# Products with v five rounds behind, another order of buffers, and side pieces from round 6 on

## The chip, the core and the metric

The kernel runs on one core of one Trainium2 chip. The metric is the time on the device in microseconds (us), as the median of several executions. The core's engines work side by side, each through its own queue in order: PE (TensorE), DVE (VectorE), ACT (ScalarE), POOL (GpSimd) and SP (SyncE, which here only issues transfers).

## The reference

Two layers on N = 3327 nodes with D = 128 features and a sparse adjacency matrix adj of zeros and ones. Layer 0 is a graph attention; layer 1 is an attention for each of the D features, with 8 components per node (H = 8), and takes by far most of the time.

```python
H = X @ W.T + b;  s = H @ a_s;  r = H @ a_r
e = leaky_relu(A * s + A * r.T, 0.2)
att = softmax(where(A > 0, e, -9e15), axis=1)
x = layernorm(X + att @ H)                        # layer 0

q, k, v = ((x @ W.T).reshape(d, n, h) for W in (Wq, Wk, Wv))
a = einsum('dnh,dmh->dnm', q, k) * d ** -0.5
a = softmax(a + adj + adj, axis=2)
out = einsum('dnm,dmh->dnh', a, v)
x = layernorm(x + out.reshape(n, h * d) @ Wo.T)   # layer 1
```

## The kernel before

**Layer 1.** The features are taken four at a time (HG = 4): 32 groups. The 3327 queries are cut into 7 blocks of 476 columns (the last has 472); so there are 224 blocks, counted through. The keys are 26 tiles of 128 (or 127) rows. For each key tile the kernel computes the scores of the four features (L152, written to PSUM tiles scb that hold two features), applies the exponential and the adjacency, and multiplies with v (L956), adding up in one PSUM tile av. After the 26th key tile of a block VectorE copies av to SBUF (L966), and SP writes it out (L970).

**Two ways to the weights.** The adjacency stands in the exponent as 0 or 2. Half a key tile (two features, 952 columns) goes one of two ways. Either ScalarE takes exp of the scores from PSUM (L1172), and GpSimd multiplies the result with a factor of 1 or e squared (L1173). Or VectorE adds adjacency and scores (L1175), and ScalarE takes exp of the sum later (L991, function exp_late): in the round after the sum is complete, for the whole key tile, 1904 columns. Both write into a tile e4 of the pool sp, which has seven buffers that are given out in turn.

**Rounds.** A block has NR = 26 rounds; one round handles two halves. Three key tiles make a triple of three rounds: in the first and the second, one half goes through ScalarE and GpSimd (tile i) and one through VectorE (tile k1); in the third, both halves of tile k2 go through VectorE. I call these rounds A, B and C. Blocks alternate between two plans. An even block starts with a triple (rounds 0, 1, 2 are A, B, C) and ends with rounds 24 and 25 for the last two tiles. An odd block starts with a round of VectorE alone (round 0), its triples begin at rounds 1, 4, 7 and so on, and round 25 handles one tile alone, one half each way.

**The order of a round.** The kernel writes out the order of each engine's queue by hand (a manual schedule). A round puts on the queues: SP's adjacency loads for a later stretch (want_adj); PE's scores; at most one side piece for PE (work_tensor); the halves on ScalarE and GpSimd or on VectorE; the late exponentials that are due; the products of one key tile (function multiply); and side pieces for VectorE and GpSimd (work). The function multiply keeps a list of key tiles whose product has not been issued, and issues the oldest when there are more than LAG = 4: products run four rounds behind. So the last product of a block, and the copy L966 that follows it, are issued in round 3 of the next block. The scores of ScalarE's half use the PSUM pool pe with one buffer, those of VectorE's half the pool pd with two, av the pool pv with one.

In odd blocks the products of round 3 are issued between the two halves on VectorE:

```python
between = odd and n == LAG - 1
...
if between and h == 1:
    multiply(s, order[n])
```

**Side pieces.** Layer 0 of the other 25 row tiles and the projections of the results are cut into small pieces that run beside layer 1. They stand in two rows: "main" (products of layer 0, L241, its normalisation, and the projections to q, k, v, and the pieces of the results) and "aside" (GpSimd's weights, L308 and L317, the loads of their adjacency, and VectorE's counts, L326). Each piece has a kind: "p" for PE, "d" and "l" for VectorE, "m" for GpSimd, "x" for loads that take no slot; "n" waits for a mark that "t" sets. The functions reading and lane say in which rounds of a block a kind has a slot, for one piece each: before, PE, VectorE and GpSimd have slots in rounds 4, 7, 10 and so on (second rounds of triples), in some first and last rounds, and PE in round 3 too (in odd blocks all one later); "l" has them a round later. The function finish_to runs what is left when a group of features needs its rows.

Of the kernel before, what the change touches and what calls it, by code (L numbers as in the profile page):

```python
# [17 lines left out]
P = 128  # L18
# [29 lines left out]
def kernel(  # L48
# [29 lines left out]
    H = wqT.shape[1]  # L78
# [13 lines left out]
    kr = [FP + (i < N - FP * NT) for i in range(NT)]  # L92
# [57 lines left out]
    def special():  # L150
# [9 lines left out]
        with ExitStack() as sx, tc.manual_schedule(engines=ALL):  # L160
# [9 lines left out]
            CH = [(i, min(i + CW, NT)) for i in range(0, NT, CW)]  # L170
# [96 lines left out]
            def layer0(t, side=True, trow=None, bank=bank, held=None):  # L267
# [4 lines left out]
                r = rows[t]  # L272
                s = {"a": {}, "w": {}}
# [191 lines left out]
                for n, (i0, i1) in enumerate(CH):  # L465

                    aside.append(("n", ("P", q0 + n - 2, 0)))
                    for c0 in range(i0, i1, 3):
                        c1 = min(c0 + 3, i1)
                        aside.append(("m", lambda n=n, c0=c0, c1=c1: weigh(n, c0, c1)))  # L470
                        aside.append(("m", lambda n=n, c0=c0, c1=c1: mask(n, c0, c1)))
                    aside.append(("t", ("W", q0 + n)))
                    c = [("d", lambda n=n, h=h, k=k: count(n, h, k)) for h in range(3) for k in range(2)]
                    counts.append(c)
                    main.append(("n", ("W", q0 + n, 3)))
                    if i1 == NT:
                        main.append(("m", biased))
                    main += [("p", lambda i=i: product(i)) for i in range(i0, i1)] + [("t", ("P", q0 + n))]
                    aside.append(counts[-1])
                return loads, main + chain + [("t", ("rows", t))], aside  # L480

            def result(t):
# [116 lines left out]
                units += [("p", lambda: turn(0, 2, 0)), ("p", lambda: turn(2, 4, 2))]  # L599
                units += [("d", lambda: divided(0, 2, 0)), ("d", lambda: divided(2, 4, 2))]  # L600
                units += [("p", lambda: turn(4, 5, 0)), ("d", lambda: divided(4, 5, 0))]
                units += [("p", lambda h=h: project(h)) for h in range(H)]
                root = rsqrt(s, lambda: s["st"][:r, 7:8], r)
                units += [("d", finish), ("d", together(variance, *root[:3]))]
                return units + [("d", together(*root[c : c + 3])) for c in (3, 6, 9)] + [("d", scale)]
# [314 lines left out]
            pd = sx.enter_context(tc.tile_pool(name="sx_sd", bufs=2, space=bass.MemoryType.PSUM))  # L920
            pe = sx.enter_context(tc.tile_pool(name="sx_se", bufs=1, space=bass.MemoryType.PSUM))
            pv = sx.enter_context(tc.tile_pool(name="sx_av", bufs=1, space=bass.MemoryType.PSUM))
            LAG = 4

# [47 lines left out]

            waiting = []

            def multiply(s, i):
                waiting.append((s, i))
                while len(waiting) > LAG:
                    products(*waiting.pop(0))  # L980

# [20 lines left out]

            def reading(n, odd):

                n -= odd
                if n % 3 == 1 and 4 <= n < NR - 2:  # L1010
                    return True
                return n in ((NR - 2,) if odd else (0, NR - 1))

            def lane(kind, n, odd):

                if kind == "l":
                    return int(reading(n - 1, odd) if n else True)
                return int(reading(n, odd) or kind == "p" and n - odd == 3)

            made = [layer0(t) for t in range(1, NT)]  # L1020
            first_loads = made[0][0]
            main = []
            aside = []
            for n, (_, m, a) in enumerate(made):

                later = []
                for u in a:
                    if u[0] == "r":

                        at = max((k for k, v in enumerate(aside) if v[0] == "n"), default=0)  # L1030
                        aside.insert(at, ("x", u[1]))
                    elif isinstance(u, list):
                        ahead = made[n + 1][0][sum(isinstance(v, list) for v in later)] if n + 1 < len(made) else None
                        later.append(u)
                        if n:
                            aside += u + [ahead] * (ahead is not None)
                    else:
                        aside.append(u)
                if n == 0:

                    for k, u in enumerate(later):
                        aside += u + [made[1][0][k]] * (len(made) > 1)
                main.append(m)
            main.append([("n", ("counts", 0, 0))] + judge())
            aside.append(("t", ("counts", 0)))
            results = [((needs[t] + 1) * total + LAG + 6, result(t)) for t in range(NT - 1)]
            end = result(NT - 1)
            marks = {("P", q): 0 for q in range(len(CH))}
            side = {"main": [], "aside": aside, "since": {"main": 0, "aside": 0}, "read": -2}

            def head(row, now, force=False):

                while True:
                    if not side[row]:
                        if row == "aside":
                            return None
                        ahead = ("rows", reads[min(max(now, 0) // total + 2, NG - 1)]) in marks
                        if results and results[0][0] <= now and (ahead or not main):
                            side[row] = results.pop(0)[1]
                        elif main:  # L1060
                            side[row] = main.pop(0)
                        else:
                            return None
                    kind, f = side[row][0]
                    if kind == "t":
                        marks[f] = now
                    elif kind == "w":
                        if not force and now - side["since"][row] < f:
                            return None
                    elif kind == "n":  # L1070
                        if f[:2] not in marks or not force and now - marks[f[:2]] < f[2]:
                            return None
                    else:
                        return kind
                    side[row].pop(0)
# [4 lines left out]

            def work_tensor(now, n, odd):

                for _ in range(lane("p", n, odd) if side["read"] != now - 1 else 0):
                    if head("main", now) != "p":
                        break
                    run("main", now)

            def work(now, n, odd):
                room, low, pool = lane("d", n, odd), lane("l", n, odd), lane("m", n, odd)
                for row in ("main", "aside"):  # L1090
                    while True:
                        kind = head(row, now)
                        if kind == "x":
                            pass
                        elif kind == "d" and room:
                            room -= 1
                            if row == "main":
                                side["read"] = now
                        elif kind == "l" and low:
                            low -= 1  # L1100
                            side["read"] = now
                        elif kind == "m" and pool:
                            pool -= 1
                        else:
                            break
                        run(row, now)

            def finish_to(mark, now):
                while mark not in marks:
                    row = "main" if head("main", -1 if now is None else now, True) else "aside"  # L1110
                    if head(row, -1 if now is None else now, True) is None:
                        break
                    run(row, -1)
                    tick(True)
# [13 lines left out]
            for g in range(NG):  # L1128
                k4, v4, _ = group
                for b in range(NBLK):  # L1130
# [5 lines left out]
                    for n, rnd in enumerate(rounds):  # L1136
# [22 lines left out]
                            for t in range(2):  # L1159
                                pair_scores(sc[i, h][: kr[i], t, :w], s.k4, s.q4, i, kr[i], 2 * h + t, w)  # L1160
                        work_tensor(g * total + at, n, odd)
                        between = odd and n == LAG - 1
                        for (i, h, at_) in rnd:
                            if between and h == 1:
                                multiply(s, order[n])
                            r, z = kr[i], sc[i, h]
                            if i not in s.e:
                                s.e[i] = sp.tile([P, HG, WB], F32, name="e4")
                            eh = s.e[i][:r, 2 * h : 2 * h + 2, :w]
                            ah = a[:r, at_ or 0, :w].unsqueeze(1).to_broadcast([r, 2, w])  # L1170
                            if at_ is None:
                                nc.scalar.activation(eh, z[:r, :, :w], AF.Exp, scale=2.0)  # L1172
                                nc.gpsimd.tensor_tensor(eh, eh, ah, op=ALU.mult)  # L1173
                            else:
                                nc.vector.tensor_tensor(eh, z[:r, :, :w], ah, op=ALU.add)  # L1175
                                added.setdefault(i, []).append(h)
# [5 lines left out]
                        if n + 1 in starts or n + 1 == NR:  # L1182
                            del adjs[m]
                            make_factor(m + 1)
                        if not between:
                            multiply(s, order[n])
                        work(g * total + at, n, odd)
            exp_late(NG * total + 2)
            finish_to(None, NG * total + LAG + 6)
# [384 lines left out]
```

## Time and profile before

| | before |
|---|---|
| median of 3 runs | 10047.68 us (10047.55 to 10053.35) |
| profiled execution, its own time | 10052.42 us |
| its span | 10050.6 us |
| first exponential of layer 1 starts | at 66.3 us |
| last exponential of layer 1 ends | at 10025.3 us |
| granted TensorE clock, mean | 0.995 |
| stretch from 114 to 167 us (53 us), busy: PE, DVE, ACT, POOL | 41.9, 40.1, 45.8, 51.2 us |
| stretch from 4972 to 5017 us (45 us), the same | 43.0, 39.9, 44.8, 44.4 us |

The page gives each engine's busy time and its share of the span, and then groups of instructions: line, engine and operation, output and inputs by name, shape and count; behind the bar the busy time in us and the mean ns of one, then the idle time of the engine before them and what ended most of it. A line of waits gives who waited for whom, the sum in us, how often, and the longest. A line of the timeline gives start, duration, engine, line, operation, names, shapes and how many instructions were merged, and in brackets the idle time before it and what ended it. A busy share counts overlapping instructions once.

### The profile page before, as it was taken

Reading aid. Unit: us, or ns where it says so; the run is one execution under the profiler, and the core shown is the slowest. Engines: PE = TensorE matmul, PEld = TensorE weight load, DVE = VectorE, ACT = ScalarE, POOL = GpSimd, SP = SyncE. Lnnn points to the kernel's source line nnn. Section 1 sums busy time; section 2 is a strip of 40 time slices with the busy share of each in tenths; the row PEclk is TensorE's granted clock in tenths of the full one; section 3 lists DMA queues with packets and bytes.
Section 4 is the critical chain, followed back from the end, with each engine's and each line's share of the span. In section 5 each row is a group of like instructions: output and inputs, shape, how many; then the busy total and the mean of one; then the engine's idle time right before and its main releaser. Section 6 shows DMA issues by size and latency. Waiting matters only on the chain.

```text
span 10050.6 us, 207550 instructions
## 1 busy us (share of the span) xinstructions
PE 9477.4 (94%) x79523; PEld 3013.9 (30%) x79523; DVE 9188.5 (91%) x10554; ACT 9897.6 (98%) x7904; POOL 9177.2 (91%) x4954
## 2 busy tenths in 40 slices
PE   7999999999999999999999999999999999999998
PEld 2233333333233233323333333333333233222222
DVE  7899999999999999999999999999999999888888
ACT  7999999999999999999999999999999999999998
POOL 7999999999999999999999999999999999888887
PEclk9999999999999999999999999999999999999999
DMA  6765656665665656565566656566665565555554
GB/s 194 209 179 179 179 168 183 178 176 168 181 173 171 183 167 189 168 184 170 169 179 187 176 172 179 176 170 178 181 179 175 171 175 168 169 158 166 164 164 132
DMA packets 1399414, 1755.28 MB, mean 175 GB/s; under 512 B 349360, under 2 KB 1386890, under 8 KB 1394312
## 3 DMA queue, kind: packets, MB, share of 16 engines
q1 hardware_dynamic: 1388061, 1739.30, 59.7%
q8 instruction: 626, 10.26, 0.4%
q10 hardware_dynamic: 10347, 2.61, 0.1%
q14 instruction: 380, 3.11, 0.1%
HBM read 1637.49 MB, written 103.93 MB: 173 GB/s over the span
## 4 chain that ended last, share of the span: by engine, by line
ACT 41%; PE 21%; POOL 16%; issue 13%; DVE 7%; DMA 2%; SPq 1%; POOLq 0%; ACTq 0%; DVEq 0%
ACT e L991 29%; POOL e L1173 15%; ACT e L1172 11%; PE av L956 11%; PE scb L152 9%; DVE e L1175 5%; PE bank L241 1%; DVE o L966 1%; DMA q4b<-qT 1%; DMA at<-in_adjT_dram 1%; POOL w L308 0%; SPq L733 0%; POOL w L317 0%; DMA k4b<-kT 0%; POOL at L793 0%
## 5 line engine op out<-in xcount | busy, mean ns | idle before, releaser
L1173 POOL TENSOR_TENSOR e<-e,at 128x952 f32<-128x952 f32 (+1 forms) x3920 | 8715.9, 2236 | 788.6 <-ACT e L1172 735.1
L1175 DVE TENSOR_TENSOR e<-scb,at 128x952 f32<-128x952 f32 (+1 forms) x7728 | 8499.4, 1142 | 769.7 <-PE scb L152 650.1
L991 ACT ACTIVATE e<-e 128x1904 f32<-128x1904 f32 (+3 forms) x3920 | 7095.9, 1810 | 26.4 <-DVE e L1175 11.1
L956 PE MATMUL av<-e,v4b 128*32 128x476 f32 (+1 forms) x46592 | 5843.8, 573 | 99.0 <-DVE o L966 68.0
L152 PE MATMUL scb<-q4b,k4b 32*128 32x476 f32 (+1 forms) x23296 | 3882.4, 486 | 440.8 <-ACT e L1172 361.9
L1172 ACT ACTIVATE e<-scb 128x952 f32<-128x952 f32 (+1 forms) x3920 | 3921.1, 1000 | 74.9 <-PE scb L152 36.7
L152 PEld LDWEIGHTS scb<-q4b,k4b 32*128 32x128 f32 (+1 forms) x23296 | 1779.3, 189 | 5459.2 <-ACT e L1172 3161.5
L956 PEld LDWEIGHTS av<-e,v4b 128*32 128x32 f32 (+1 forms) x46592 | 1014.1, 109 | 1239.9 <-issue 933.4
L241 PE MATMUL bank<-hsb,w 128*32 128x129 f32 (+1 forms) x5200 | 278.6, 286 | 0.0
L326 DVE TENSOR_SCALAR_CACHE_REDUCE dump<-a 128x384 bf16<-128x384 f32 (+2 forms) x468 | 247.3, 528 | 0.6
L308 POOL TENSOR_SCALAR w<-trow,er 128x129 f32<-128x129 f32 x650 | 231.6, 376 | 1.3
L317 POOL TENSOR_TENSOR w<-w,a 128x384 f32<-128x384 f32 (+3 forms) x225 | 207.9, 924 | 0.1
L966 DVE COPY o<-av 128x476 f32<-128x476 f32 (+1 forms) x224 | 145.2, 648 | 31.3 <-PE av L956 30.4
L241 PEld LDWEIGHTS bank<-hsb,w 128*32 128x32 f32 (+1 forms) x5200 | 102.9, 108 | 148.2 <-issue 148.2
L241 PE MATMUL bank<-wo,ot 128*32 128x128 f32 x1600 | 85.2, 285 | 0.0
L402 DVE TENSOR_SCALAR hi<-bank 128x256 fp32r<-128x256 f32 (+1 forms) x200 | 83.0, 415 | 0.0
L409 DVE SCALAR_TENSOR_TENSOR lo<-bank,hi 128x256 fp32r<-128x256 f32 (+1 forms) x200 | 83.0, 415 | 0.0
L241 PE MATMUL bank<-wk,x1T 128*32 128x256 f32 x800 | 63.9, 391 | 0.0
L241 PE MATMUL bank<-wq,x1T 128*32 128x256 f32 x800 | 63.9, 391 | 0.0
L241 PE MATMUL bank<-wv,x1T 128*32 128x256 f32 x800 | 63.9, 391 | 0.0
L502 PE MATMUL bank<-ident,o 128*128 128x128 f32 x225 | 52.0, 304 | 0.0
L290 POOL MEMSET a<- 128x128 f32 (+1 forms) x25 | 5.2, 208 | 44.4 <-DVE dump L326 44.4
(123 smaller groups left out, 647.3 us busy)
## 6 DMA issues: line engine op xcount, KB each, us to landing
at<-in_adjT_dram SPq DMA_DIRECT2D x1536, 476.0 KB
at<-ftd SPq DMA_DIRECT2D x1674, 238.0 KB
at<-in_adjT_dram SPq DMA_DIRECT2D x256, 472.0 KB
at<-ftd SPq DMA_DIRECT2D x279, 236.0 KB
k4b<-kT SPq DMA_DIRECT2D x128, 415.9 KB
q4b<-qT SPq DMA_DIRECT2D x1528, 29.8 KB
at<-in_adjT_dram SPq DMA_DIRECT2D x192, 208.2 KB
at<-in_adjT_dram SPq DMA_DIRECT2D x150, 238.0 KB
```

The costliest lines, as they stand in the source:

```text
L152: nc.tensor.matmul(dst, k4[32 * j : 32 * j + H4, first_key(i) : first_key(i) + 2 * r - 1 : 2], q4[32 * j : 32 * j + H4, :nb], start=True, ...
L241: nc.tensor.matmul(dst[c0:c1], w[:, c0:c1], mov, **kw)
L308: nc.gpsimd.tensor_scalar(w, s["t"][:, :, :T3], -LOWEST, e, op0=ALU.min, op1=ALU.max)
L317: nc.gpsimd.tensor_tensor(w, w, s["a"][n][:, c0 - i0 : c1 - i0, :r], op=ALU.mult)
L326: nc.vector.tensor_scalar(z, a, float(k), None, op0=ALU.is_equal, op1=ALU.add, accum_out=even[:, t, at : at + 1])
L402: nc.vector.tensor_scalar(hi[:r, o : o + QW], s["b"][:r, :QW], scale, None, op0=ALU.mult)
L956: nc.tensor.matmul(s.av[32 * j : 32 * j + 32, : s.w], s.v4[:r, j, i * H1 : i * H1 + 32], e[:r, j, : s.w], start=(s.left == NT - 1), stop=( ...
L966: nc.vector.tensor_copy(o4[:, :w], s.av[:, :w])
L991: nc.scalar.activation(e, e, AF.Exp, scale=2.0)
L1172: nc.scalar.activation(eh, z[:r, :, :w], AF.Exp, scale=2.0)
L1173: nc.gpsimd.tensor_tensor(eh, eh, ah, op=ALU.mult)
L1175: nc.vector.tensor_tensor(eh, z[:r, :, :w], ah, op=ALU.add)
```

## The change

Five things are changed.

1. LAG is 5. The pool of e4 tiles keeps its seven buffers.
2. In a round the e4 tile of VectorE's half is taken from the pool ahead of that of ScalarE's half.
3. The function multiply issues one product per round, but two in round 25 of odd blocks, down to four waiting; in round 0 of even blocks four wait, and in round 1 none is issued. The rule "between" is gone: the last product of a block and the copy L966 are issued in round 4, behind the halves of that round, in both kinds of blocks.
4. Side pieces have no slot below round 6 (7 in odd blocks), but for "l" in round 0. From there VectorE and GpSimd have one slot in each second round of a triple, "l" one in each third. Products of layer 0 and projections of the results get a kind of their own, "q", with slots in the first and the second round of each triple. Round 25 of odd blocks has slots for all kinds but "l".
5. The counts and the loads of later adjacency chunks become a third row, "counts", behind "main" and "aside", so that GpSimd's pieces no longer stand behind VectorE's; a mark ("L") makes GpSimd's pieces wait until their chunk's load has been issued. The counts of the first tile are no longer held back.

```diff
-                    main += [("p", lambda i=i: product(i)) for i in range(i0, i1)] + [("t", ("P", q0 + n))]
+                    main += [("q", lambda i=i: product(i)) for i in range(i0, i1)] + [("t", ("P", q0 + n))]
...
-            LAG = 4
+            LAG = 5
...
-            def multiply(s, i):
-                waiting.append((s, i))
-                while len(waiting) > LAG:
-                    products(*waiting.pop(0))
+            def multiply(n, odd):
+
+                k, lag = 1, LAG
+                if odd and n == NR - 1:
+                    k, lag = 2, LAG - 1
+                elif n == 0 and not odd:
+                    lag = LAG - 1
+                elif n == 1 and not odd:
+                    k = 0
+                for _ in range(k):
+                    if len(waiting) > lag:
+                        products(*waiting.pop(0))
...
-            def reading(n, odd):
+            def lane(kind, n, odd):
 
                 n -= odd
-                if n % 3 == 1 and 4 <= n < NR - 2:
-                    return True
-                return n in ((NR - 2,) if odd else (0, NR - 1))
-
-            def lane(kind, n, odd):
-
-                if kind == "l":
-                    return int(reading(n - 1, odd) if n else True)
-                return int(reading(n, odd) or kind == "p" and n - odd == 3)
+                if n == NR - 2 and odd:
+                    return int(kind != "l")
+                if kind == "l" and n == -1:
+                    return 1
+                if n < 6:
+                    return int(kind == "l" and n == 0 and not odd)
+                return int(n % 3 == {"q": 0, "l": 2}.get(kind, 1) or n % 3 == 1 and kind == "q")
...
-                        later.append(u)
-                        if n:
-                            aside += u + [ahead] * (ahead is not None)
+                        counts += u
+                        if n + 1 < len(made):
+                            counts += [("n", ("W", (n + 1) * len(CH) + k, 0)), made[n + 1][0][k], ("t", ("L", (n + 2) * len(CH) + k))]
+                        k += 1
...
-                for row in ("main", "aside"):
+                for row in ("main", "aside", "counts"):
...
-                        between = odd and n == LAG - 1
-                        for (i, h, at_) in rnd:
-                            if between and h == 1:
-                                multiply(s, order[n])
-                            r, z = kr[i], sc[i, h]
+                        for i, _, _ in reversed(rnd):
                             if i not in s.e:
                                 s.e[i] = sp.tile([P, HG, WB], F32, name="e4")
+                        for i, h, at_ in rnd:
+                            r, z = kr[i], sc[i, h]
...
-                        if not between:
-                            multiply(s, order[n])
+                        waiting.append((s, order[n]))
+                        multiply(n, odd)
                         work(g * total + at, n, odd)
```

More of the change, by code (lines that the diff above doesn't have):

```diff
@@ L467, in layer0 @@
                     aside.append(("n", ("P", q0 + n - 2, 0)))
+                    aside.append(("n", ("L", q0 + n, 0)))
                     for c0 in range(i0, i1, 3):
@@ L601, in result @@
                 units += [("p", lambda: turn(4, 5, 0)), ("d", lambda: divided(4, 5, 0))]
-                units += [("p", lambda h=h: project(h)) for h in range(H)]
+                units += [("q", lambda h=h: project(h)) for h in range(H)]
                 root = rsqrt(s, lambda: s["st"][:r, 7:8], r)
@@ L1022, in special @@
             main = []
-            aside = []
+            aside, counts = [], []
             for n, (_, m, a) in enumerate(made):
-                later = []
+                k = 0
                 for u in a:
                     if u[0] == "r":
-                        at = max((k for k, v in enumerate(aside) if v[0] == "n"), default=0)
+                        at = max((k for k, v in enumerate(aside) if v[0] == "n" and v[1][0] == "P"), default=0)
                         aside.insert(at, ("x", u[1]))
                     elif isinstance(u, list):
-                        ahead = made[n + 1][0][sum(isinstance(v, list) for v in later)] if n + 1 < len(made) else None
-                        later.append(u)
-                        if n:
-                            aside += u + [ahead] * (ahead is not None)
+                        counts += u
+                        if n + 1 < len(made):
+                            counts += [("n", ("W", (n + 1) * len(CH) + k, 0)), made[n + 1][0][k], ("t", ("L", (n + 2) * len(CH) + k))]
+                        k += 1
                     else:
                         aside.append(u)
-                if n == 0:
-                    for k, u in enumerate(later):
-                        aside += u + [made[1][0][k]] * (len(made) > 1)
                 main.append(m)
             main.append([("n", ("counts", 0, 0))] + judge())
-            aside.append(("t", ("counts", 0)))
+            counts.append(("t", ("counts", 0)))
             results = [((needs[t] + 1) * total + LAG + 6, result(t)) for t in range(NT - 1)]
@@ L1048, in special @@
             marks = {("P", q): 0 for q in range(len(CH))}
-            side = {"main": [], "aside": aside, "since": {"main": 0, "aside": 0}, "read": -2}
+            marks.update({("L", len(CH) + k): 0 for k in range(len(CH))})
+            side = {"main": [], "aside": aside, "counts": counts, "since": {}, "read": -2}
             def head(row, now, force=False):
@@ L1054, in head @@
                     if not side[row]:
-                        if row == "aside":
+                        if row != "main":
                             return None
@@ L1081, in work_tensor @@
             def work_tensor(now, n, odd):
-                for _ in range(lane("p", n, odd) if side["read"] != now - 1 else 0):
-                    if head("main", now) != "p":
-                        break
+                kind = head("main", now)
+                if kind in ("p", "q") and lane(kind, n, odd) and side["read"] != now - 1:
                     run("main", now)
@@ L1109, in finish_to @@
                 while mark not in marks:
-                    row = "main" if head("main", -1 if now is None else now, True) else "aside"
-                    if head(row, -1 if now is None else now, True) is None:
+                    at = -1 if now is None else now
+                    row = next((row for row in ("main", "aside", "counts") if head(row, at, True)), None)
+                    if row is None:
                         break
```

## The prediction

> **What bounds the kernel now.** I read the page first: busy times, then the groups.
>
> ```profile
> PE 9477.4 (94%) x79523; PEld 3013.9 (30%) x79523; DVE 9188.5 (91%) x10554; ACT 9897.6 (98%) x7904; POOL 9177.2 (91%) x4954
> ...
> L1173 POOL TENSOR_TENSOR e<-e,at 128x952 f32<-128x952 f32 (+1 forms) x3920 | 8715.9, 2236 | 788.6 <-ACT e L1172 735.1
> L1175 DVE TENSOR_TENSOR e<-scb,at 128x952 f32<-128x952 f32 (+1 forms) x7728 | 8499.4, 1142 | 769.7 <-PE scb L152 650.1
> L991 ACT ACTIVATE e<-e 128x1904 f32<-128x1904 f32 (+3 forms) x3920 | 7095.9, 1810 | 26.4 <-DVE e L1175 11.1
> ...
> L1172 ACT ACTIVATE e<-scb 128x952 f32<-128x952 f32 (+1 forms) x3920 | 3921.1, 1000 | 74.9 <-PE scb L152 36.7
> ```
>
> ScalarE is the bound: 98% busy, and the change leaves its 7840 exponentials alone. So a gain can come only out of ScalarE's delays. I call L1172 (exp from the scores; POOL's L1173 multiplies its result) S, VectorE's add L1175 V, the late exp L991 E. The waits of ScalarE alone name little:
>
> ```profile
> ACT e L1172 <- PE scb L152: 36.7, 32, 4.9
> ACT e L1172 <- DVE e L1175: 22.7, 1, 22.7
> ACT e L991 <- DVE e L1175: 11.1, 32, 1.0
> ```
>
> They miss short delays, because two undisturbed activations overlap. The timeline shows more: from start to start an S takes 0.843 us and an E 1.682 us (medians over all of them). A pair of blocks (even, odd) holds 35 S, 34 E and one half E of 0.888: 35 x 0.843 + 34 x 1.682 + 0.888 = 87.6 us; by the starts a typical pair takes 88.56. So 1.0 us per pair, 112 pairs, is delay. Summing each start's excess over those medians by round: 165 us in all, in even blocks 29 before round 3's S, 19 before round 5's E, 35 before round 6's S; in odd blocks 37 before round 4's E; rounds 7 to 25 together about 16. Two timelines show why; first an even block (round 3 begins at 4976.08):
>
> ```profile
> 4976.08 0.96 ACT L1172 ACTIVATE e<-scb 128x952 f32<-128x952 f32 x1
> ...
> 4977.91 0.64 DVE L966 COPY o<-av 128x476 f32<-128x476 f32 x1
> ...
> 4978.61 1.01 PE L956 MATMUL av<-e,v4b 128*32 128x476 f32 x8 [0.24 <-DVE o L966]
> ...
> 4979.70 1.79 ACT L991 ACTIVATE e<-e 128x1904 f32<-128x1904 f32 x1
> ...
> 4981.63 0.97 ACT L1172 ACTIVATE e<-scb 128x952 f32<-128x952 f32 x1
> ```
>
> The block before ends its av in round 3. The copy L966 stands on VectorE ahead of round 4's V, whose E then starts at 4979.70, 0.19 late (the S before it began at 4978.67, 0.84 more is 4979.51). The first product of the new block waits for the copy, the scores behind it on PE come late, and round 6's S starts at 4981.63 instead of 4979.70 + 1.68 = 4981.38: 0.25 late. Now an odd block, where the copy stands between round 3's two V:
>
> ```profile
> 5021.36 0.65 DVE L966 COPY o<-av 128x476 f32<-128x476 f32 x1 [0.15 <-PE av L956]
> ...
> 5021.93 3.23 DVE L1175 TENSOR_TENSOR e<-scb,at 128x944 f32<-128x944 f32 x3
> 5022.00 1.08 ACT L1172 ACTIVATE e<-scb 128x944 f32<-128x944 f32 x1
> ...
> 5023.15 1.78 ACT L991 ACTIVATE e<-e 128x1888 f32<-128x1888 f32 x1
> ```
>
> The second V starts at 5021.93, ends 1.13 later, and its E starts at 5023.15, not at 5022.84: 0.31 late, as in most odd blocks.
>
> **What the Trainium skill says.** "ScalarE: Activation LUTs", section "What ACT_TABLE_LOAD costs", gives 186 ns + 0.833 ns per column with an overlap of about 93 ns back to back: 1679 ns for 1904 columns; the trace has 1682. "TensorE: Matmul & The Clock Gate", "The mechanism", says matmuls start and end strictly in program order; the trace agrees with it in every round that I listed. "Perfetto Trace Analysis", "Identifying the Most-Contended Engine", says matmul busy time is a poor measure; so PE's 94% is not used below, its starts are.
>
> **The change, part by part.** (1) Products five rounds behind, the pool still seven e4 tiles. In rounds with two new tiles five wait, so all seven are taken. With V's tile taken first, tiles are taken in the order in which products free them: S's tile is then freed by the product of the round before. PE runs in order and that product stands ahead of this round's scores, which S needs anyway: cost 0. The cover is that order; were it lost, each S could wait up to one product, 0.93 us. S's product gets one more round (about 1.6 us) after POOL; PE's waits for POOL were 115 us under weight loads, little of it reaching ScalarE: gain 0 to 5, taken 0.
>
> (2) The last product of a block, and the copy with it, moves from round 3 to round 4, after its V. Odd: the two V of round 3 run on, the second ends about 5022.2 against a need of 5022.84. The copy now stands ahead of round 5's V: copy done near 5023.86, V to 5024.9, E due at 5025.37; PE's product waits about 0.37, and round 7's S is ready near 5026.9, due 5027.05. So the 37 us go and nothing takes their place. Even: round 5's E needs a V without a copy ahead, ready about 0.4 early: 17 of 19 us go (the rest is in the first blocks). Round 6's S: from the end of round 3's S, PE needs 0.07 + 0.43 (scores) + 0.93 (product) until round 5's scores, whose second pair waits for V; the first new product waits for the copy (about 2.35 after round 4's scores), then 0.93, 0.5 and 0.1: ready 5.0 to 5.1 after round 3's S starts, due at 2 x (0.843 + 1.682) = 5.05. A tie, 0 to 0.1 late, taken 0.04: of about 26 us outside the first blocks 22 go.
>
> (3) Two products in odd round 25, none in even round 1. PE has one product (0.87 to 0.93) more before even round 0. Followed from 4968.31 (round 25's scores): products at 4968.98 and 4969.85, round 0's scores 4970.8 (now 4970.24), V pair of round 1 at 4972.4, its V from 4972.9 to 4974.05, then the second pair of round 2 (it needs that PSUM buffer), product 4974.5, round 3's scores 4975.45, S ready 4976.03; due 4975.91. Late by 0.12 (now 0.17). A side product in round 25 (31 of 112 odd blocks in the new program's order) adds 0.245, a side projection (23 of 112) about twice that: mean 0.52 x 0.12 + 0.28 x 0.36 + 0.20 x 0.6 = 0.28. The present 29 us hold about 13 of single blocks with a lower granted clock, so 16/112 = 0.14 is the typical value: cost +15 us. This is the weakest step: 0 to 0.45, so -15 to +35 us.
>
> (4) Side pieces. Their number is unchanged; the order of both programs shows 850 side products, 455 other PE pieces, 1239 for VectorE, 475 for POOL, in neither bunched at a deadline. Side products now stand in rounds A and B of a triple (A, B with an S each, C without). Present PE loop of a triple with one:
>
> ```profile
> 5003.34 0.43 PE L241 MATMUL bank<-hsb,w 128*32 128x129 f32 x8
> ...
> 5003.58 0.98 PE L956 MATMUL av<-e,v4b 128*32 128x476 f32 x8
> ...
> 5007.98 0.49 PE L152 MATMUL scb<-q4b,k4b 32*128 32x476 f32 x4 [0.25 <-ACT e L1172]
> ```
>
> A side product delays what follows by 0.24 (5003.34 to 5003.58); the loop (5.05) ends in a wait of 0.25. A second one fits, with 0.01 to 0.06 left: cost 0 steadily. VectorE: 4 V at 1.06 from start to start plus a count 0.62 (or two 0.415 pieces) is 4.9 to 5.1 per triple; with 7 in place of 8.5 slots a block, and rounds below 6 free to absorb the copy: 0. SP issues the same loads; those of later adjacency chunks now follow the counts, with no consumer near: 0.
>
> (5) The first seven blocks are bound by POOL (51.2 busy of 53 in the stretch from 114 to 167 us: it also makes the factors, L793). The new order puts 35 POOL pieces there in place of 25, each about 1.0 us (three L308 of 0.37, or one L317 of 0.92). Blocks that had idle POOL take some; cost +6 (0 to +10).
>
> Sum: -37 - 17 - 22 + 15 + 6, and -7 of small ones (round 1's S 6.0, round 3's E 4.3, part of them): -62. The profiled execution took 10052.4 (span 10050.6, 1.8 around it), so 9990; the median shown is 4.7 below it: 9985.
>
> **The rivals.** Slower: PE becomes the bound, in the triples from round 6 on. About 420 triples now hold two side products, and PE's rest is 0.06 or less; if a second one pushes the next scores out in full, at 0.245 each, 420 x 0.245 = 103 is lost against the 62 won: +41, 10089. It decides from 0.15 per triple (62/420). For it: 94% busy, the loop so close. Against it: rounds with an S wait for ScalarE today, and a second product in round A comes after its S scores. Little change: the stall only moves; the copy blocks PE as long in round 4, and round 3's S is 0.45 late: -37 + 35 - 17 + 6 is -13, with half of round 5's gain lost near -5: 10040. That round 25's double product undoes nothing: round 3's delay vanishes as well, -15 in place of +15, round 6 wholly, and the longer product slack saves 10 in the first blocks: -37 - 17 - 26 - 15 + 6 - 7 - 10 = -106, 9942.
>
> **How the numbers follow.** Forecast 0.57 (9960 to 10015), all gone 0.15 (9925 to 9960), little change 0.15 (10015 to 10050), slower by PE 0.13 (10060 to 10110). Within 0.2% is 10027.6 to 10067.8, about what a measurement of this kernel can tell. Faster 0.57 + 0.15 + 0.05 = 0.77; same 0.10 + 0.01 = 0.11; slower 0.12. The range reaches from 9935 to 10035: it leaves out about 0.05 below and 0.15 above.
>
> **What would show it.** Right: in odd blocks round 4's E starts 0.84 after its S; L966 follows round 4's V; round 5's E on time; round 6's S within 0.1; a typical pair of blocks near 88.0 in place of 88.56; round 3's S still late, more after a side piece in round 25. Wrong: S waits in rounds A beyond 6 (PE is full), S's start held by a product (the seventh tile), or POOL ends round 6's product late.

## The result, and the profile after

The changed kernel takes 9985.1 us (median of 6 runs, 9983.1 to 9991.4), the kernel before 10051.3 us beside it (6 runs, 10047.6 to 10053.8): a ratio of 0.9935, 95% interval 0.9923 to 0.9948. The profiled execution has a span of 9983.4 us in place of 10050.6, so 67.2 us less. The page after:

```profile
PE 9441.9 (95%) x79523; PEld 2997.2 (30%) x79523; DVE 9189.1 (92%) x10554; ACT 9866.4 (99%) x7904; POOL 9175.6 (92%) x4954
...
L1175 POOL TENSOR_TENSOR e<-e,at 128x952 f32<-128x952 f32 (+1 forms) x3920 | 8715.4, 2238 | 720.0 <-ACT e L1174 673.0
L1177 DVE TENSOR_TENSOR e<-scb,at 128x952 f32<-128x952 f32 (+1 forms) x7728 | 8501.1, 1142 | 724.3 <-PE scb L152 518.9
L1000 ACT ACTIVATE e<-e 128x1904 f32<-128x1904 f32 (+3 forms) x3920 | 7488.3, 1910 | 10.4 <-DVE e L1177 8.8
...
L1174 ACT ACTIVATE e<-scb 128x952 f32<-128x952 f32 (+1 forms) x3920 | 4314.7, 1101 | 53.3 <-PE scb L152 25.2
```

The lines have moved by a few: L1174 is S, L1175 GpSimd's product, L1177 V, L1000 E, L957 the product with v (av), L967 the copy. Each engine has as many instructions as before. ScalarE's waits as the trace names them:

```profile
ACT e L1174 <- PE scb L152: 25.2, 32, 2.2
ACT e L1174 <- DMA v4b<-vd: 22.1, 1, 22.1
ACT hi L404 <- PE mm L199: 10.5, 3, 8.3
ACT e L1000 <- DVE e L1177: 8.8, 19, 2.0
```

In all, ScalarE's waits fell by some 13 us only (99.3 to 86.3); as before, most of the delay is in the spacing of ScalarE's starts. With the medians of the kernel before (S 0.843, E 1.682), the excess over them by round, in us, for blocks 8 to 223:

| | before | after |
|---|---|---|
| even, round 0's S | 0.0 | 6.0 |
| even, round 1's S | 0.0 | 3.4 |
| even, round 3's S | 28.3 | 8.8 |
| even, round 3's E | 4.2 | 1.2 |
| even, round 5's E | 18.2 | 0.0 |
| even, round 6's S | 25.5 | 0.8 |
| odd, round 4's E | 35.4 | 0.1 |
| all rounds from 8 on | 3.7 | 13.7 |
| all rounds | 125.3 | 48.6 |
| a typical pair of blocks, length | 88.56 | 87.88 |
| blocks 0 to 7, length | 384.1 | 392.3 |

So blocks 8 to 223 give 77 us less of delay, the first eight blocks take 8.2 us more, and the start of layer 1 (67.9 in place of 66.3) and the tail make up the rest of the 67.2. That start lies between 65.1 and 69.4 us over the runs below, so its 1.6 us are not put down to the change.

The timeline of an even block after (the first ACT line is round 2's E, the second round 3's S, the third round 4's S):

```profile
4945.58 0.48 PE L152 MATMUL scb<-q4b,k4b 32*128 32x476 f32 x2 [0.56 <-DVE e L1177]
4945.71 1.97 ACT L1000 ACTIVATE e<-e 128x1904 f32<-128x1904 f32 x1
...
4947.52 1.02 ACT L1174 ACTIVATE e<-scb 128x952 f32<-128x952 f32 x1
...
4950.06 1.00 ACT L1174 ACTIVATE e<-scb 128x952 f32<-128x952 f32 x1
4950.23 0.64 DVE L967 COPY o<-av 128x476 f32<-128x476 f32 x1
...
4950.90 1.85 ACT L1000 ACTIVATE e<-e 128x1904 f32<-128x1904 f32 x1
4950.93 0.16 PEld L957 LDWEIGHTS av<-e,v4b 128*32 128x32 f32 x8 [0.37 <-DVE o L967]
...
4952.58 1.02 ACT L1174 ACTIVATE e<-scb 128x952 f32<-128x952 f32 x1
```

The copy now runs while round 5's E has already all it needs: the E starts at 4950.90, 0.84 after round 4's S. PE still waits for the copy with its first product of the new block (0.37), but the S of round 6 starts at 4952.58, just 1.68 after the E. What is left is round 3's S: it starts 1.81 after round 2's E, so 0.13 late, behind scores of round 2 that waited for V (the first line; see step 3 below). An odd block:

```profile
4992.95 1.14 ACT L1174 ACTIVATE e<-scb 128x944 f32<-128x944 f32 x1
4993.78 1.97 ACT L1000 ACTIVATE e<-e 128x1888 f32<-128x1888 f32 x1
4994.14 0.20 PEld L152 LDWEIGHTS scb<-q4b,k4b 32*128 32x128 f32 x4 [1.29 <-ACT e L1174]
4994.14 0.49 PE L152 MATMUL scb<-q4b,k4b 32*128 32x472 f32 x4 [0.45 <-ACT e L1174]
4994.23 0.64 DVE L967 COPY o<-av 128x476 f32<-128x476 f32 x1
...
4994.92 1.00 PE L957 MATMUL av<-e,v4b 127*32 127x472 f32 x8 [0.29 <-DVE o L967]
```

Round 4's E starts 0.83 after its S, and the copy comes after that, with a short wait of PE (0.29) that nobody on ScalarE sees.

### The profile page after: what moved, and what is told of

It reads as the page before. It is cut to its first block, busy times and chain, and to the rows that moved or that the text cites. A ratio compares the mean times of both kernels' runs of the same rounds, so it can differ in the third digit from the quotient of the medians.

```text
span 9983.4 us, 207568 instructions
## 1 busy us (share of the span) xinstructions
PE 9441.9 (95%) x79523; PEld 2997.2 (30%) x79523; DVE 9189.1 (92%) x10554; ACT 9866.4 (99%) x7904; POOL 9175.6 (92%) x4954
## 4 chain that ended last, share of the span: by engine, by line
ACT 43%; PE 30%; issue 10%; POOL 10%; DVE 5%; DMA 1%; SPq 0%; POOLq 0%; DVEq 0%; ACTq 0%
ACT e L1000 31%; PE av L957 15%; PE scb L152 12%; ACT e L1174 12%; POOL e L1175 9%; DVE e L1177 4%; PE bank L241 2%; DVE o L967 1%; DMA at<-in_adjT_dram 1%; POOL w L308 0%; POOL w L317 0%; POOL at L794 0%; DVE lo L409 0%; DMA at<-ftd 0%; DVE dump L326 0%
## 5 line engine op out<-in xcount | busy, mean ns | idle before, releaser
L1175 POOL TENSOR_TENSOR e<-e,at 128x952 f32<-128x952 f32 (+1 forms) x3920 | 8715.4, 2238 | 720.0 <-ACT e L1174 673.0
L1177 DVE TENSOR_TENSOR e<-scb,at 128x952 f32<-128x952 f32 (+1 forms) x7728 | 8501.1, 1142 | 724.3 <-PE scb L152 518.9
L1000 ACT ACTIVATE e<-e 128x1904 f32<-128x1904 f32 (+3 forms) x3920 | 7488.3, 1910 | 10.4 <-DVE e L1177 8.8
L957 PE MATMUL av<-e,v4b 128*32 128x476 f32 (+1 forms) x46592 | 5815.9, 573 | 77.8 <-DVE o L967 36.8
L1174 ACT ACTIVATE e<-scb 128x952 f32<-128x952 f32 (+1 forms) x3920 | 4314.7, 1101 | 53.3 <-PE scb L152 25.2
L152 PEld LDWEIGHTS scb<-q4b,k4b 32*128 32x128 f32 (+1 forms) x23296 | 1746.4, 189 | 5403.3 <-ACT e L1174 3189.4
L957 PEld LDWEIGHTS av<-e,v4b 128*32 128x32 f32 (+1 forms) x46592 | 1030.0, 108 | 1244.3 <-issue 1011.5
L326 DVE TENSOR_SCALAR_CACHE_REDUCE dump<-a 128x384 bf16<-128x384 f32 (+2 forms) x468 | 247.3, 528 | 0.6
L967 DVE COPY o<-av 128x476 f32<-128x476 f32 (+1 forms) x224 | 144.1, 643 | 7.4 <-PE av L957 7.3
```

The source lines that it names most:

```text
L152: nc.tensor.matmul(dst, k4[32 * j : 32 * j + H4, first_key(i) : first_key(i) + 2 * r - 1 : 2], q4[32 * j : 32 * j + H4, :nb], start=True, ...
L326: nc.vector.tensor_scalar(z, a, float(k), None, op0=ALU.is_equal, op1=ALU.add, accum_out=even[:, t, at : at + 1])
L957: nc.tensor.matmul(s.av[32 * j : 32 * j + 32, : s.w], s.v4[:r, j, i * H1 : i * H1 + 32], e[:r, j, : s.w], start=(s.left == NT - 1), stop=( ...
L967: nc.vector.tensor_copy(o4[:, :w], s.av[:, :w])
L1000: nc.scalar.activation(e, e, AF.Exp, scale=2.0)
```

## The experiments

Theory "copy": the gain comes from the place of the last product and of the copy behind it. Rival "slots": it comes from first rounds without side pieces. All times are medians; the kernel before, on the same chips, took 10047.8 (e1 to e4), 10048.1 (e5 to e8) and 10048.3 (e9 to e12). Below, "delay" is that of the table above, in blocks 8 to 223.

**e1, the products part alone.** The kernel before with the new multiply, LAG = 5, the new order of tiles and no "between"; its slots as they were.

```diff
-            LAG = 4
+            LAG = 5
...
-            def multiply(s, i):
+            def multiply(n, odd):
...
+                if odd and n == NR - 1:
+                    k, lag = 2, LAG - 1
```

> The products part alone (lag five, V's tile first, two products in odd round 25, last product and copy in round 4), on the kernel before with its old slots for side pieces. Theory 'copy' (the gain is the place of the last product and of the copy): odd round 4's E is on time (35 us of delay gone), even round 5's E too (18 gone), the first eight blocks stay at 384 us; total 9980 to 10005. Theory 'slots' (the gain is that the first rounds are free of side pieces): 10040 to 10050, the delays before rounds 3 to 6 stay.

Measured: 10023.1, ratio 0.9976 (0.9968 to 0.9984). The mechanism of "copy" is there, its size is not: odd round 4's E is on time (0.0), even round 5's E nearly (4.1), round 6's S at 9.4, the first eight blocks take 382.5. But even round 2's E is now late by 22.3 in sum and round 3's S by 35.8. The total lies between the two expected ranges: both missed.

**e2, the side-piece part alone.** The changed kernel with LAG = 4, the old multiply, the old order of tiles and the "between" rule.

```diff
-            LAG = 5
+            LAG = 4
...
+                        between = odd and n == LAG - 1
```

> The side-piece part alone (new slots, third row for the counts), with lag four, the old function multiply, the copy between the halves of odd round 3. Theory 'copy': odd round 4's E stays 0.3 late and even round 5's E 0.19 late, the first eight blocks take 8 us more: 10035 to 10060. Theory 'slots': 9985 to 10005.

Measured: 10057.2, ratio 1.0008 (1.0002 to 1.0015). The steady delays are those of before (even round 3's S 27.9, round 5's E 17.9, round 6's S 25.1, odd round 4's E 33.7), the first eight blocks take 394.8, 10.7 more than before, which covers the loss of 9. So clear first rounds win nothing by themselves; the two parts need each other: -25 and +9 alone, -64 together.

**e3, one product in every round.**

```diff
-                if odd and n == NR - 1:
-                    k, lag = 2, LAG - 1
-                elif n == 0 and not odd:
-                    lag = LAG - 1
-                elif n == 1 and not odd:
-                    k = 0
```

> The changed kernel with one product in every round (no second product in odd round 25, none left out in even round 1). My prediction's step 3 (the double product costs 15 us in even round 3): about 9970, even round 3's S nearly on time. The rival (leaving out round 1's product is what brings round 3's S forward): even round 3's S back to 0.17 late or more (+10 to +20), rounds 0 and 1 lose their 9 us of delay, total 9985 to 9995.

Measured: 9992.3, 0.9945 (0.9928 to 0.9961). Even round 3's S is back at 28.0, round 0's S at 0.0, round 3's E at 4.3. The rival holds: moving round 1's product to round 25 wins 19 in round 3 and costs 6 in round 0. My step 3 had the wrong sign.

**e4, only the last product one round later.** The kernel before, LAG = 4 and old slots, with the new order of tiles and no "between"; no product in round 3, one in round 4, two in round 5.

```diff
+                for _ in range({LAG - 1: 0, LAG + 1: 2}.get(n, 1)):
+                    if len(waiting) > LAG:
+                        products(*waiting.pop(0))
```

> The kernel before with lag four and old slots, where only round 3 of every block issues no product, round 4 one (the last of the block before, then the copy) and round 5 two. Theory 'copy': odd round 4's E and even round 5's E on time, about 50 us gone; round 5's two products cost PE 0.9 us once a block and may bring new delay before round 6 or 7: 9985 to 10020. Rival 'depth' (the gain comes from one more round for POOL's products everywhere): 10040 to 10050.

Measured: 10144.9, 1.0098 (1.0081 to 1.0115), far outside both. The two E are on time (-0.1 and 1.0, of 18 and 35), but round 6's S of even blocks is 92 late in sum, round 7's S of odd blocks 67. The timeline of one even block shows why:

```profile
5029.92 1.80 PE L956 MATMUL av<-e,v4b 128*32 128x476 f32 x16
...
5031.65 0.49 PE L152 MATMUL scb<-q4b,k4b 32*128 32x476 f32 x4
...
5032.27 0.97 ACT L1171 ACTIVATE e<-scb 128x952 f32<-128x952 f32 x1 [0.72 <-PE scb L152]
```

The two products of round 5 stand on PE in front of the scores that the next S needs, after a wait for the copy: in the median 0.81 us before round 6 of an even block, 0.55 before round 7 of an odd one. It is the price of catching up right there; a lag of five avoids it by not catching up until round 25.

**e5 and e6, slots given back in the first rounds,** for PE (e5) or for VectorE (e6) alone, in the changed kernel.

```diff
                 if n < 6:
+                    if kind in ("p", "q"):
+                        return int(n in (3, 4) or n == 0 and not odd)
...
+                    if kind == "d":
+                        return int(n == 4 or n == 0 and not odd)
```

> The changed kernel with PE's slots of before given back in the first rounds (rounds 3 and 4, in odd blocks 4 and 5, and round 0 of even blocks), VectorE's and GpSimd's left as they are. The first experiments: products alone won 24, slots alone nothing, both 65, so the two parts work together in even blocks. If it is PE's pieces there: even rounds 2, 3 and 6 get the delay of the products-only kernel (22, 36 and 9 us), total 10010 to 10025. If it is VectorE's pieces: no more than 10 us lost, 9985 to 9995.

> The changed kernel with VectorE's slots of before given back in the first rounds (round 4, in odd blocks 5, and round 0 of even blocks), PE's and GpSimd's left as they are. If it is VectorE's pieces that must be out of the way: round 2's E late (22 us), round 5's or 6's E and S late, total 10010 to 10025. If it is PE's: 9985 to 9995.

Measured: e5 10013.3, 0.9963 (0.9949 to 0.9977); e6 10038.1, 0.9991 (0.9984 to 0.9998). VectorE's pieces cost 53 us, PE's 28; both more than the "no more than 10" that each was to cost where the other was the cause. e5's total lies in the range for PE, though its delays are smaller than expected (10, 15 and 3 in even rounds 2, 3 and 6, not 22, 36 and 9); e6's lies outside both of its ranges. The two costs can't be added: they make 81, while e1, with all the old slots, is only 38 slower than the changed kernel. In e6 even round 2's E is late by 14.4 and round 3's S by 40.6. One block of e6:

```profile
4977.22 0.54 DVE L326 TENSOR_SCALAR_CACHE_REDUCE dump<-a 128x384 bf16<-128x384 f32 x1
...
4977.69 3.25 DVE L1179 TENSOR_TENSOR e<-scb,at 128x952 f32<-128x952 f32 x3
...
4978.89 0.51 PE L152 MATMUL scb<-q4b,k4b 32*128 32x476 f32 x2 [0.87 <-DVE e L1179]
...
4979.33 1.82 PE L957 MATMUL av<-e,v4b 128*32 128x476 f32 x8
...
4981.94 0.96 ACT L1176 ACTIVATE e<-scb 128x952 f32<-128x952 f32 x1 [1.22 <-PE scb L152]
```

A count (L326) issued in round 0 stands ahead of round 1's V. Round 2's second pair of scores needs the PSUM buffer that this V reads, so PE rests 0.87 us (it has no product in round 1). And then the products take 1.82 in place of 1.01 us: the clock was halved. The stretches around show it (the columns are the stretch and its length, then busy time of PE, weight load, VectorE, ScalarE and GpSimd with instruction counts, the granted clock and the DMA share):

```profile
4972.40:4975.80 3.40, 3.40 (x40) 1.22 (x32) 3.23 (x5) 3.40 (x3) 3.40 (x5) 1.00 0.92 345
4975.80:4979.20 3.40, 2.53 (x20) 0.85 (x16) 3.04 (x5) 3.40 (x5) 3.40 (x4) 1.00 0.74 222
4979.20:4982.60 3.40, 3.40 (x22) 0.69 (x20) 2.37 (x3) 2.18 (x2) 3.40 (x3) 0.50 0.72 217
```

A stretch of 3.4 us in which PE was 74% busy is followed by one at half the clock, and S waits 1.22. The steady part (420 to 9940 us) of e6 has 28 such changes with 96 us at half the clock, e1 has 20 with 85, e5 8 with 34, the changed kernel 1 with 3.4, and before 6 with 20. From such a change until 3 us after it ends, the starts of ScalarE are late by 0.7 to 1.7 us, 32 in sum over e6's 28 changes, 26 of them beyond the median delay of the same rounds. That is about half of the 48 us of delay that e6 has more than the changed kernel (97 against 49). The rest comes at full clock, from the late V itself: in the median block round 3's S is 0.22 late, in place of 0.04.

PE's busy share alone doesn't tell when the clock goes down. In the 3.41 us ahead of the 28 changes it was 46 to 78%; but here is a stretch of e6 with 70% that was followed by full clock:

```profile
2228.09:2231.50 3.41, 2.38 (x24) 0.95 (x20) 2.78 (x5) 3.28 (x5) 3.41 (x5) 1.00 0.59 153
2231.50:2234.92 3.42, 3.26 (x30) 0.96 (x34) 3.05 (x3) 3.30 (x3) 3.42 (x4) 1.00 0.79 256
```

**e7, ScalarE's tile first again.**

```diff
-                        for i, _, _ in reversed(rnd):
+                        for i, _, _ in rnd:
```

> The changed kernel with ScalarE's half taking its e4 tile ahead of VectorE's again. My step 1 (the order is what makes lag five free): VectorE's tile is then the one freed by a product that is issued in the same round, behind this round's scores, so each V of a first round waits for about a product (0.9 us more): VectorE has 0.2 us or less of rest per triple after a side piece, so 10050 to 10300, with VectorE's adds waiting for PE's products. Rival (the order of tiles doesn't matter): 9985, no such wait.

Measured: 9982.6, 0.9935 (0.9918 to 0.9951), with the delays of the changed kernel round by round (even round 3's S 10.7, all 48.6). The order of tiles doesn't matter; my reason in step 1 falls. With seven buffers given out strictly in turn, V of a first round would have waited for a product here, and the trace names no wait of V for one. So that reading of the pool doesn't hold; the runs don't show how the buffers are given out instead.

**e8 and e11, two attempts at a better version.** e11 takes PE's side pieces out of odd round 25; e8 does that too, and holds back GpSimd's pieces in the first group:

```diff
-                    return int(kind != "l")
+                    return int(kind in ("d", "m"))
...
-                        elif kind == "m" and pool:
+                        elif kind == "m" and pool and not (row == "aside" and now < total - NR and ("W", 2 * len(CH) - 1) in marks):
```

> An attempt at a better version: the changed kernel where (a) GpSimd's side pieces beyond the first tile wait until the last block of the first group, so that 26 in place of 35 fall into the seven blocks that GpSimd bounds, and (b) odd round 25, with its two products, has no side piece on PE. If GpSimd bounds the first blocks as I said: they take about 9 us less (383 in place of 392). If a side piece in round 25 is what delays even round 0 (6 us) and part of round 3's S (9 us): some 8 us less. Together 9965 to 9975; the rival, that nothing of this matters: 9985.

> The changed kernel without PE's side pieces in odd round 25 alone (one part of the last attempt). If they are what delays even rounds 0 and 3: these two lose some 11 us, the first eight blocks stay at 392, total 9972 to 9980; else 9985.

Measured: e8 9981.8 (0.9933, 0.9917 to 0.9950), e11 9985.2 (0.9936, 0.9919 to 0.9952). Neither reaches the total hoped for (9965 to 9975, and 9972 to 9980). In both, even round 0's S is on time (0.3 and 0.2) and round 3's S at 3; but in odd blocks round 6's E and round 7's S have 9 and 8 in place of 2.5 and 2.3, nearly all in a handful of blocks with the clock halved (15 of 18 us in e8, 14 of 15 in e11). The first eight blocks of e8 take 387.8 in place of 392.3 (e11: 392.7): GpSimd's pieces there cost half of what I had expected.

**e9, VectorE's slot in round 4 only,** not in round 0.

```diff
+                    if kind == "d":
+                        return int(n == 4)
```

> The changed kernel with VectorE's side slot given back in round 4 (5 in odd blocks) only, not in round 0 of even blocks. In the kernel with both back, a count in even round 0 stood ahead of round 1's V, whose PSUM buffer round 2's scores need; PE then rested and its clock was halved for 3.4 us. If that one place is the cause: 9983 to 9992, and no half clock in the steady part. If round 4 matters as well (it is where the copy stands): 10005 to 10030.

Measured: 9981.7, 0.9934 (0.9917 to 0.9951); half the clock once in the steady part, as in the changed kernel. So the whole 53 us of e6 come from one slot, VectorE's piece in round 0 of even blocks: by the late V and by the halved clock, about half each.

**e10, side products in all three rounds of a triple.**

```diff
-                return int(n % 3 == {"q": 0, "l": 2}.get(kind, 1) or n % 3 == 1 and kind == "q")
+                return int(kind == "q" or n % 3 == {"l": 2}.get(kind, 1))
```

> The changed kernel with side products allowed in all three rounds of a triple, to see where PE fills up: the loop of a triple with three is 4.99 + 0.245 = 5.23 against ScalarE's 5.05. Rival 'PE is the bound' of my prediction: new delays before S in first rounds beyond 6, 0.18 per full triple, some 100 to 200 such triples: 10005 to 10025. If PE has more rest than I counted: 9985 to 9992.

Measured: 9979.0 (9976.9 to 9981.5), 0.9932 (0.9915 to 0.9948), below both expected ranges, although the program has 217 triples with three side pieces on PE. The rounds from 8 on have 19 of delay in place of 12 to 14, not the 39 of 217 x 0.18. PE isn't full at two, and hardly at three.

**e12, the changed kernel again.**

> The changed kernel once more, on the same chip as the three others, for comparison: 9985.

Measured: 9984.6 (9982.9 to 9985.6), 0.9937 (0.9920 to 0.9953). Beside it on the same chip e10 is 5.7 us (0.06%) faster, with ranges that don't overlap; that is less than I trust a difference of two kernels to be. No version beats the changed kernel by more than that.

Two parts of the change were not tried alone: GpSimd's slots in the first rounds, and the third row "counts". What they give by themselves is open.

## Why the prediction was right, point by point

**The bound, and where a gain can come from: right.** ScalarE does the same work. Blocks 8 to 222 take 9452.7 in place of 9529.2 us, and those 76.5 us are the 76.7 of delay before ScalarE's starts that are gone; the waits by name show few of them.

**Step 1, five rounds behind at no cost: the number right, the reason not.** No S was held by a product: ScalarE's waits name none. The reason given, that tiles must be taken in the order in which products free them, is refuted by e7. PE's weight loads wait 20 us for GpSimd's products after 400 us in place of 73, as foreseen with no visible gain. Not foreseen: V waits 61 us for GpSimd in place of 14.5; what lies behind it wasn't tried, and E isn't late by it.

**Step 2, the copy in round 4: right.** Foreseen -37, -17 and -22; measured -35, -18 and -25 in the steady blocks. e1 and e4, two other kernels with the copy behind round 4's halves, both free these two E; e4 shows that it is the place of the copy and not the depth of the lag. The tie in round 6 came out at 0.00 in the median, in place of 0.04.

**Step 3, two products in round 25: wrong in sign.** Foreseen +15 in round 3; measured -19.5 there and +9.4 in rounds 0 and 1, so -10, and e3 puts the whole at -8. About 10 of the 19.5 stood in the six blocks of the kernel before in which the clock was halved just there, and there is none such after; in the median block the delay went from 0.17 to 0.04. The failing step is the spacing: I let round 0's two pairs of scores follow 0.25 us apart and the product start 0.67 after the first, as in the trace of before. In the trace after, all four matmuls of a round whose buffers are free go out together, and the product follows 0.42 after them:

```profile
4942.48 0.49 PE L152 MATMUL scb<-q4b,k4b 32*128 32x476 f32 x4
4942.90 0.16 PEld L957 LDWEIGHTS av<-e,v4b 128*32 128x32 f32 x8 [0.23 <-issue]
```

From there round 1's V, and the S of round 3, come 0.25 to 0.33 earlier than I had them: 0.13 late in the block shown (with a side piece in round 25), not 0.36. In the trace of before the pairs stood apart because the second needed a PSUM buffer that V was still reading: in the round that I followed, V ended at 4968.50 and the second pair began at 4968.56. The trace names such a wait in round 3 of the same block:

```profile
4975.93 0.19 PEld L152 LDWEIGHTS scb<-q4b,k4b 32*128 32x128 f32 x2 [0.25 <-DVE e L1175]
```

With two products in round 25, PE comes to round 0 later, when V has finished (in the block shown at 4942.16, ahead of the scores at 4942.48).

**Step 4, side pieces at no cost: nearly right for PE, incomplete for the rest.** The rounds from 8 on have 10 us more of delay than before. The slower rival, PE as the bound with two side products in 420 triples (368 by the trace), foresaw 103 there; it is refuted by the result, and once more by e10. What the text didn't say is what the clear first rounds are worth: without them the other part wins 25 and not 64 (e1). The costliest slot found is VectorE's in even round 0 (e6 against e9), about half of it through the halved clock that follows.

**Step 5, GpSimd in the first blocks: right.** Foreseen +6, measured +8.2; with nine pieces fewer there (e8) 4.5 of it go.

**The sum.** Foreseen -62 for the profiled execution, measured -67: step 3 gave 25 more than I had it, step 2 another 2; against that stand the 10 lost in later rounds, 10 of small terms (7 foreseen as gain; with the later start of layer 1 they cost 3), and 2 more in the first blocks. That the total came so close is in part luck: the errors, 27 one way and 22 the other, nearly cancel. That 9985 is the measured median to the unit is luck too: it was counted from a median before of 10047.7 (three runs), which is 10051.3 over the six. One rival's sum has a slip ("little change" comes to 10043, not 10040); nothing rests on it.

## What to carry to other kernels

Where the bounding engine is 98% busy, look at the spacing of its starts by place in the loop: delays of 0.2 us, hidden by overlap from a view of waits, made up nearly all that was won here. The copy that empties av at the seam of two blocks belongs behind the work that the next step of the bound needs, and its engine must have slack just there: here the same move cost 1% when PE caught up in the wrong round, won 0.25% with side work left in the way, and 0.65% with both cleared.

## What the runs showed of the hardware

A rest of PE of less than 1 us, which left it 74% busy over 3.4 us, was followed by 3.4 us at half the clock (one block of e6, with 28 such changes in the steady part), each with 0.7 to 1.7 us of delay on ScalarE. The Trainium skill ("TensorE: Matmul & The Clock Gate", "What's actually happening") speaks of an idle window of about 3.4 us; the length agrees with the trace (3.41), but here stretches in which PE was three quarters busy were followed by the half clock, though not all of them. What decides between them is open. And recorded durations are no price: from the kernel before to the changed one the mean of E went from 1810 to 1910 ns and that of S from 1000 to 1101, while the spacing of undisturbed starts stayed at 1.68 and 0.84 us.
